# Attention and depthwise convolution, fused: the last image's tail re-planned

## The chip, the cores and the metric

The kernel runs on one core of one Trainium2 chip. The metric is the device time of one execution in microseconds (us); all times here are in us unless ns is written. Engines are called as the profile calls them: PE is TensorE, PEld its weight load, DVE is VectorE, ACT is ScalarE, POOL is GpSimd and SP is SyncE, which here only issues DMAs. L601 is line 601 of the kernel.

## The reference

There are 16 images of 384 channels and 32 x 32 pixels, all float32. Two layers are applied, each as "add to the input":

```
x = x + attention(groupnorm(x))      # 8 heads of 48 channels, 1024 tokens, softmax, projection + bias
x = x + dwconv7x7(groupnorm(x))      # depthwise, weights made symmetric over four rotations, padding 3
```

Group normalization has 32 groups of 12 channels, so each image needs a mean and a variance per group before either layer can start on it. The 7 x 7 depthwise convolution is 49 taps per channel: for each tap the shifted image, times one weight per channel, is added to an accumulator.

## The kernel before

**Layout.** Channels lie on partitions, 128 at a time, so an image is three channel blocks, k = 0, 1, 2, each a tile of 128 x 1024 (32 rows of 32). A tile is written (b, k) here: (14, 2) is block 2 of image 14. `x1[b,k]` is the image after attention and also the accumulator of the convolution; `xn1[b,k]` is its normalized copy, which the taps read.

**Stages.** PE does the attention of image b: q and k (L416), v (L442), scores (L467), weighted sums (L483), projection (L536; in the last image L573). ACT takes the exponentials and evicts. DVE does, meanwhile, the convolution of image b-1 as a chain of taps (L601, one `scalar_tensor_tensor` each). A tile's 49 taps are a *chain*; up to three chains are active and their taps alternate. A program written by hand orders everything: the loop over images issues PE's steps and advances `clock`, an estimate of PE's time; `catch_up(clock)` then places DVE's work until its estimate, `vclock`, has reached `clock`. Due work is kept in a heap (`after(wait, cost, f)`), and what is left of the time is filled with taps, each counted by `us_tap` (L821). Each engine executes its instructions strictly in that order. `us_tap` adds 0.02 to each tap while the last image is in work.

**Statistics for the second normalization.** For images 0 to 13 ACT computes them: `x1_means` (one small DVE instruction, L944), three `Square` activations (`x1_squares`, L265), a gather through DRAM, an aggregate on DVE (L277), `Ln` and `Exp` on ACT, and a spread through DRAM. For image 14 (`ON_VECTOR`, L912) DVE does it: six `bn_stats` (L234), then an aggregate and 14 small instructions (L247 to L222). For image 15, the last, `groups_on_pe` (L290) averages over groups by matmuls with 128 x 1 operands: first `average` of the means (14 PE records, L302), three small DVE instructions (L315 to L317), a second `average` of the variances (14 records), then DVE (L320), POOL's power (L322) and DVE (L323). A callback, `between`, puts one tap on DVE after each average. After that `x1_chains` normalizes the tiles of image 15, (15,2) on DVE, (15,1) on ACT and (15,0) on POOL, and stores two of them to DRAM (`xd`, L676).

**Convolution on PE.** When attention is done PE is free, so some tiles of the last two images (`PE_TILES`) get their taps on PE: (14,2), (14,1), (15,2) and (15,1). The rows come back from DRAM as tiles `sh` (`conv_load`, L683: four DMAs of 160 KB a tile, two tiles for each half of 16 output rows). A half is two pieces (`conv_piece`, L1107) of 56 PE records each (L707): seven taps, four groups of 32 columns side by side, two records per matmul. When a tile is through, DVE adds the result from PSUM (L722). Tile (14,1) is `SHARED`: DVE does its first `SPLIT` = 24 rows and PE the other 8. Tile (15,0) stays on DVE entirely, in two sums (`sum2`, L854), joined at L862. `sh` tiles share a pool of five buffers with `qk`; one of the five holds PE's second set of weights.

**The end of the program.** In the last image the reciprocal of the softmax sums is taken directly (`divide_at_once`, L564, multiply at L565); `fast_finish` then issues the last projection part (L573), adds the residual (L582) and takes `bn_stats`. Then come one piece of (14,2), `fast_end` (the averages and the normalization), and a loop over the pieces that are left: three of (14,2), two of (14,1), four of (15,2), four of (15,1). Before the pieces of image 15 a small matmul checks the softmax sums' range (`check_tensor`, L1093), and DVE reads its result (`good`, L1095). `loads(n)` issues the next `sh` tiles in the order of `pe_loads`, when a piece has ended a half.

Of the kernel before, what the change touches and what calls it, by code (L numbers as in the profile page):

```python
# [44 lines left out]
def kernel(  # L45
# [27 lines left out]
    B, C, H, W = x.shape  # L73
# [36 lines left out]
    def run(general):  # L110
        tag = "g" if general else "f"
        with ExitStack() as stack:
# [24 lines left out]
            xds, shs, pss, mats, psums = {}, {}, {}, {}, {}  # L137
# [1 line left out]

            PE_TILES = [(b, k) for b in (B - 2, B - 1) for k in PE_K]  # L140
            SHARED = None if general else (B - 2, PE_K[1])
            SPLIT = 3 * H // 4
            LONE = (B - 1, 0)

            def flat(t):
# [81 lines left out]
            class Stats:  # L227
# [59 lines left out]
                    )  # L287
                    self.spread(af)

                def groups_on_pe(self, masks, between=lambda: None):  # L290

                    st = small.tile([P, NK, 2], F32, tag="st", name=f"st_{self.name}")
                    for k in range(NK):
                        nc.vector.bn_aggr(st[:, k, :], self.bs[:, k, :])
                    ps = ps_o.tile([P, HALF], F32, tag="acc", name=f"ps_st_{self.name}")

                    def average(c0, src):
                        for mo in range(NK):
                            blocks = [n for n, b in enumerate(MASK_BLOCKS) if b[1] == mo]
                            for n in blocks:  # L300
                                ki = MASK_BLOCKS[n][0]
                                nc.tensor.matmul(  # L302
                                    ps[:, c0 + mo : c0 + mo + 1],
                                    lhsT=masks[:, n, :],
                                    rhs=src[:, ki : ki + 1],
                                    start=(n == blocks[0]),
                                    stop=(n == blocks[-1]),
                                )

                    mean = small.tile([P, NK], F32, tag="mn", name=f"mn_{self.name}")  # L310
                    nc.vector.tensor_copy(mean, st[:, :, 0])
                    average(0, mean)
                    between()
                    d = small.tile([P, NK], F32, tag="d", name=f"d_{self.name}")
                    nc.vector.tensor_tensor(d, mean, ps[:, 0:NK], ALU.subtract)  # L315
                    nc.vector.tensor_tensor(d, d, d, ALU.mult)
                    nc.vector.tensor_tensor(d, d, st[:, :, 1], ALU.add)  # L317
                    average(NK, d)
                    between()
                    nc.vector.tensor_scalar(d, ps[:, NK : 2 * NK], EPS, None, ALU.add)  # L320
                    self.sc = small.tile([P, NK, 2], F32, tag="sc", name=f"sc_{self.name}")
                    nc.gpsimd.tensor_tensor(self.sc[:, :, 0], d, mhalf[:, 0:NK], ALU.pow)  # L322
                    nc.vector.scalar_tensor_tensor(  # L323
                        self.sc[:, :, 1], ps[:, 0:NK], -1.0, self.sc[:, :, 0], ALU.mult, ALU.mult
                    )
# [493 lines left out]
                heapq.heappush(later, (now() + wait, count, cost, f))  # L819

            def us_tap(dy, dx):  # L821
                late_us = 0.02 if clock > last_image else 0.0
                rows = H - abs(dy)
                if tuple(active[0][0:2]) == SHARED:
                    rows = min(H - max(0, dy), SPLIT) - max(0, -dy)
                return (rows * (W - abs(dx)) + (128 if len(active) > 1 else 268)) / 955 + late_us
# [57 lines left out]
            chunks, proj = deque(), deque()  # L884
            ready = {}
            x1_stats = {}
            pe_conv, pe_loads = deque(), deque((bk, h, a) for bk in PE_TILES for h in range(bk == SHARED, 2) for a in range(2))

            def issue(c):
                nonlocal clock  # L890
# [18 lines left out]
            lims = []  # L909

            applies = deque()
            ON_VECTOR = (B - 2,)  # L912

            def project(b):
                nonlocal clock
# [185 lines left out]
            def loads(n):  # L1101
                while n and pe_loads and pe_loads[0][0] in xn1s:
                    (b, k), h, a = pe_loads.popleft()
                    conv_load(b, k, h, a)
                    n -= 1

            def conv_piece():  # L1107
                nonlocal clock
                b, k, h, part = pe_conv.popleft()
                while (b, k, h, 1) not in shs:  # L1110
                    loads(1)
                conv_on_pe(b, k, h, part)
                clock += 3.2 if (b, k) == SHARED else 6.2
                if part == 1:
                    loads(2)
                if (h, part) == (1, 1):
                    after(6.0, 1.2, lambda: conv_on_pe_end(b, k))
# [29 lines left out]
                vclock = clock + 4.0  # L1147

            def fast_end(b):
                x1_stats[b].groups_on_pe(late["masks"], tap)  # L1150
                x1_chains(b, x1_stats[b])

            def once(key, when):
# [5 lines left out]
            for b, n0, size in [  # L1159
                (b, b * PER_B + sum(SIZES[:g]), SIZES[g]) for b in range(B) for g in range(len(SIZES))  # L1160
            ]:
                r = n0 - b * PER_B
                if n0 == NS - PER_B:
                    last_image = clock
                if r % (2 * NT) == 0 and r // (2 * NT) < NK:
                    while chunks and chunks[0][1:] <= (b, r // (2 * NT)):
                        issue(chunks.popleft())
                for n in range(n0, n0 + size):
                    s_step(n)
                clock += (size * US_STEP + US_TURN) / 2  # L1170
                if r == 0:
                    for i in range(NT // 2):
                        issue(("v", b, i))
                ending = b == B - 1 and r + size == PER_B
                if ending:
                    catch_up(clock)
                    divide_at_once(NP * b + NP - 1, 0)
                    vclock += 4.2
                    for o in range(NK):
                        proj_part(b, o, (0, 1))  # L1180
                    clock += 2 * US_PROJ
                else:
                    catch_up(clock)
                    act_slot(4.5)
                    other(n0 + size, False)
                for n in range(n0, n0 + size):
                    av_step(n)
                    u, h, i = n // (2 * NT), n // NT % 2, n % NT
                    if i == NT - 1:
                        take(u, h)  # L1190
                clock += (size * US_STEP + US_TURN) / 2
                if n0 // (2 * NT) < (n0 + size) // (2 * NT):
                    finish((n0 + size) // (2 * NT) - 1)
                if ending:
                    catch_up(clock)
                    assert not invs and not waiting
                    fast_finish(b)
                else:
                    other(n0 + size, True)
                if b == B - 4 and r == 32:  # L1200
                    after(0.0, 2.0, check_early)
                if b == 1 and r == 0:
                    conv_prepare()
                if b == B - 1:

                    if once("mat_0", r >= 16):
                        mat = flat2(xpool.tile([P, NK, N], F32, tag="x", name="mat_0"))
                        conv_matrices(0, mat)
                        late["w3"] = mat[:, 2 * SH * KS * CH :][:, 0:C]
                    if once("w", r >= 32 and b - 1 in x1_stats):  # L1210
                        nc.sync.dma_start(wp, w4[:, 0:NK])
                        nc.sync.dma_start(late["w3"], w4[:, NK])
                    if once("mat_1", r >= 24):
                        conv_matrices(1, flat2(qkpool.tile([P, 2, N], F32, tag="qk", name="mat_1")))
                    if once("ones", r >= 32):
                        t = opool.tile([P, N], F32, tag="o", name="masks_1")
                        nc.sync.dma_start(t, masks.rearrange("p b c -> p (b c)"))
                        late["masks"] = t.rearrange("p (b c) -> p b c", c=P)
                if b == B - 1:
                    if r >= 32 and (b, 0) not in x1s and all(c[0] > b - 2 for c in active):  # L1220
                        for k in range(NK):
                            x1s[b, k] = rpool.tile([P, N], F32, tag="x1", name=f"x1_{b}_{k}")
                            nc.gpsimd.dma_start(
                                x1s[b, k], x[b, k * P : (k + 1) * P].rearrange("p h w -> p (h w)")
                            )
                if b == B - 1 and r in (32, 40, 48):
                    loads(1)
# [63 lines left out]
```

## Time and profile before

| | |
|---|---|
| median of 3 runs | 2943.15 (2942.83 to 2946.42) |
| the profiled execution | 2937.9, of which the span is 2935.8 |
| busy in the span | PE 2905.3, DVE 2572.6, ACT 1435.2, POOL 193.6 |
| last reciprocal (DVE L564) starts | 2828.37 |
| last join of a PE tile (DVE L722) starts | 2922.78 |

Times inside the program are counted from the span's start. The shares of busy time are averages over 16 images; the change lies in the last image and a half, so the timeline there is what has to be read. PE's records in a piece overlap, since the four column groups run side by side.

### The profile page before, as it was taken

The page shows a single profiled execution, that of the slowest core. Times are in us where ns is not written, and L with a number is a line of the kernel's source. Part 1 is how long each engine was busy: PE and PEld are TensorE (multiplying, and loading weights), DVE is VectorE, ACT ScalarE, POOL GpSimd, SP SyncE. Part 2 cuts the span into 40 slices and gives each one's busy share as a digit, 9 for nine tenths or more (in the row PEclk, how much of TensorE's full clock was granted, in tenths as well). Part 3 has the DMA queues.
Part 4 walks back from the last instruction along what each step waited for, and adds up shares of the span by engine and source line. Part 5 has one row for each costly group of instructions (what it writes and reads, how often), then busy time and mean ns, then how long its engine had stood idle before and what let it go on. Part 6 is the DMA issues. An engine that isn't in the chain of part 4 may idle for free. (4 is left out here: it accounts for less than half of the span.)

```text
span 2935.8 us, 30304 instructions
## 1 busy us (share of the span) xinstructions
PE 2905.3 (99%) x11554; PEld 1186.4 (40%) x11554; DVE 2572.6 (88%) x2565; ACT 1435.2 (49%) x1713; POOL 193.6 (7%) x305
## 2 busy tenths in 40 slices
PE   8999999999999999999999999999999999999998
PEld 4343343434434343343434434343343434334335
DVE  4413998989999898989989899898999989899996
ACT  2545445464554545546464554546545365553510
POOL 2113000000100001000000100000010000100000
PEclk9999999999999999999999999999999999999999
DMA  6423022220302213022221301213031221301424
GB/s 234 152 54 70 16 37 68 42 62 23 82 16 42 69 26 79 16 49 55 42 63 26 86 16 35 69 31 73 16 67 38 42 64 26 84 16 35 120 64 111
DMA packets 72540, 169.86 MB, mean 58 GB/s; under 512 B 30416, under 2 KB 32352, under 8 KB 70848
## 3 DMA queue, kind: packets, MB, share of 16 engines
q0 software_dynamic: 29456, 96.10, 13.0%
q1 hardware_dynamic: 41168, 68.12, 9.6%
q10 hardware_dynamic: 1760, 3.61, 0.5%
q8 instruction: 93, 1.52, 0.2%
q14 instruction: 63, 0.52, 0.1%
HBM read 119.93 MB, written 29.36 MB: 51 GB/s over the span
## 5 line engine op out<-in xcount | busy, mean ns | idle before, releaser
L601 DVE SCALAR_TENSOR_TENSOR x<-xn,wsym,x 128x899 f32<-128x899 f32 (+11 forms) x2181 | 2363.9, 1156 | 103.6 <-ACT xn L333 102.7
L475 ACT ACTIVATE e<-ps_s 128x1024 f32<-128x1024 f32 x1024 | 952.4, 1051 | 54.8 <-PE ps_s L467 51.9
L467 PE MATMUL ps_s<-qk 48*128 48x512 f32 x4096 | 915.0, 596 | 1.2 <-ACT qk L423 1.1
L483 PE MATMUL acc<-e,v 128*64 128x512 f32 x4096 | 907.2, 595 | 0.0
L467 PEld LDWEIGHTS ps_s<-qk 48*128 48x128 f32 x4096 | 375.5, 185 | 536.9 <-ACT e L475 259.9
L483 PEld LDWEIGHTS acc<-e,v 128*64 128x64 f32 x4096 | 283.0, 137 | 608.3 <-issue 600.0
L416 PE MATMUL ps_qk<-x,wqk 128*128 128x512 f32 x1152 | 507.1, 596 | 2.4 <-DVE x L329 2.4
L494 ACT COPY o<-acc 128x512 f32<-128x512 f32 x128 | 75.2, 588 | 614.5 <-PE acc L483 614.5
L416 PEld LDWEIGHTS ps_qk<-x,wqk 128*128 128x128 f32 x1152 | 216.8, 190 | 289.0 <-issue 286.5
L442 PE MATMUL ps_v<-wv,x 128*128 128x384 f32 x768 | 252.0, 488 | 0.0
L536 PE MATMUL ps_proj<-o,wp 128*128 128x512 f32 x540 | 234.5, 593 | 0.6 <-DMA o<-o 0.6
L423 ACT COPY qk<-ps_qk 128x1024 f32<-128x1024 f32 x96 | 96.5, 1007 | 248.5 <-PE ps_qk L416 248.4
L442 PEld LDWEIGHTS ps_v<-wv,x 128*128 128x128 f32 x768 | 144.6, 190 | 109.7 <-ACT e L475 12.1
L551 POOL DMA_DIRECT2D x<-in_x x45 | 39.2, 870 | 1864.6 <-ACT x L544 1731.4
L519 DVE TENSOR_TENSOR o<-o,inv 128x1024 f32<-128x1024 f32 x63 | 76.8, 1218 | 88.6 <-DMA inv<-inv 69.7
L536 PEld LDWEIGHTS ps_proj<-o,wp 128*128 128x128 f32 x540 | 102.3, 190 | 127.6 <-issue 123.5
L451 ACT COPY v<-ps_v 128x384 f32<-128x384 f32 x128 | 55.1, 483 | 185.6 <-PE ps_v L442 185.6
L544 ACT ACTIVATE x<-ps_proj,bp 128x1024 f32<-128x1024 f32 x45 | 50.2, 1115 | 184.0 <-PE ps_proj L536 184.0
L333 ACT ACTIVATE xn<-x,sc_x 128x1024 f32<-128x1024 f32 x46 | 53.8, 1231 | 91.2 <-DMA sc_x<-gr_x 62.1
L508 DVE RECIPROCAL rec<-sums 128x16 f32<-128x16 f32 x63 | 15.2, 241 | 77.6 <-DMA sums<-sum 77.6
L707 PE MATMUL ps_conv<-sh,mat 128*32 128x480 f32 (+7 forms) x784 | 78.2, 551 | 1.8 <-DVE good L1095 1.3
L356 DVE BATCH_NORM_STATS2 bs_all<-xs 128x6 f32<-128x512 f32 x84 | 51.9, 679 | 13.5 <-DMA xs<-in_x 13.5
(113 smaller groups left out, 518.5 us busy)
## 6 DMA issues: line engine op xcount, KB each, us to landing
x<-in_x POOLq DMA_DIRECT2D x90, 512.0 KB, 5.6
inv<-inv SPq DMA_DIRECT2D x126, 256.0 KB
out<-x POOLq DMA_DIRECT2D x48, 512.0 KB, 7.4
xs<-in_x POOLq DMA_DIRECT2D x42, 512.0 KB, 6.1
qk<-qk SPq DMA_DIRECT2D x96, 128.0 KB
o<-o SPq DMA_DIRECT2D x90, 64.0 KB
sh<-xd SPq DMA_DIRECT2D x34, 160.0 KB
sh<-xd ACTq DMA_DIRECT2D x22, 160.0 KB
```

The costliest lines, as they stand in the source:

```text
L416: nc.tensor.matmul(ps[:, h, :], lhsT=wqk[:, k, s, t, :], rhs=xns[b][:, k, h * HALF : (h + 1) * HALF], start=(k == 0), stop=(k == NK - 1),)
L423: nc.scalar.copy(halves(qks[u][:, s, :]), ps)
L442: nc.tensor.matmul(ps[:, j, 0:C], lhsT=xns[b][:, k, t * P : (t + 1) * P], rhs=wv[:, k, :], start=(k == 0), stop=(k == NK - 1),)
L451: nc.scalar.copy(dst.rearrange("p (h d) -> p h d", d=D + 1)[:, :, 0:D], ps[:, j, 0:C].rearrange("p (h d) -> p h d", d=D),)
L467: nc.tensor.matmul(ps[:, j, :], lhsT=qks[u][r, 1, i * P : (i + 1) * P], rhs=qks[u][r, 0, h * HALF : (h + 1) * HALF], start=True, stop=True,)
L475: nc.scalar.activation(es[n], ps, AF.Exp, scale=SCALE)
L483: nc.tensor.matmul(accs[u, h][64 * j : 64 * j + 64, :], lhsT=v_of(u, i, j), rhs=e[:, j, :], start=(i == 0), stop=(i == NT - 1),)
L494: nc.scalar.copy(os_[u][:, h * HALF : (h + 1) * HALF], accs.pop((u, h)))
L519: nc.vector.tensor_tensor(os_[u], os_[u], invs.pop(u), ALU.mult)
L536: nc.tensor.matmul(ps[:, h, :], lhsT=wp[:, t, o * P : (o + 1) * P], rhs=os_[NP * b + t][:, h * HALF : (h + 1) * HALF], start=(t == 0), sto ...
L601: nc.vector.scalar_tensor_tensor(acc, xn1s[b, k].rearrange("p (h w) -> p h w", w=W)[:, iy, ix], wsym[:, k, dy + PAD, dx + PAD : dx + PAD + 1],
L707: nc.tensor.matmul(pss[b, k][CH * i : CH * (i + 1), h, :].rearrange("p (y x) -> p y x", x=W)[:, y0:, ox], lhsT=mats[k][:, i, d0 * KS + dx ...
```

## The change

It has five parts. (1) The surcharge per tap in `us_tap` in the last image is 0.045 instead of 0.02, so that the planner counts each tap longer and places fewer of them ahead of each due step. (2) `ON_VECTOR` is empty: image 14's statistics take the way of images 0 to 13, over ACT. (3) `SPLIT` is 28 rows: DVE does 28 rows of tile (14,1) and PE 4. (4) PE's two pieces of (14,1) move: one between the two averages of image 15 (`on_pe`), one right after the second average, ahead of the normalization. (5) The `sh` tiles of (14,1) are loaded first, and a fourth tile is loaded before the last unit's weighted sums (`loads(1)`) and not after it; a planned piece of (14,1) counts 2.0 instead of 3.2.

```
-            SPLIT = 3 * H // 4
+            SPLIT = 7 * H // 8
...
-                def groups_on_pe(self, masks, between=lambda: None):
+                def groups_on_pe(self, masks, between=lambda: None, on_pe=lambda: None):
...
                     average(0, mean)
+                    on_pe()
                     between()
...
-                late_us = 0.02 if clock > last_image else 0.0
+                late_us = 0.045 if clock > last_image else 0.0
...
-            pe_conv, pe_loads = deque(), deque((bk, h, a) for bk in PE_TILES for h in range(bk == SHARED, 2) for a in range(2))
+            pe_conv, pe_loads = deque(), deque(
+                (bk, h, a)
+                for bk in sorted(PE_TILES, key=lambda t: t != SHARED)
+                for h in range(bk == SHARED, 2)
+                for a in range(2)
+            )
...
-            ON_VECTOR = (B - 2,)
+            ON_VECTOR = ()
...
-            def conv_piece():
+            def conv_piece(n=0):
                 nonlocal clock
-                b, k, h, part = pe_conv.popleft()
-                while (b, k, h, 1) not in shs:
+                b, k, h, part = pe_conv[n]
+                del pe_conv[n]
+                while (b, k, h, 1) not in shs and pe_loads:
                     loads(1)
                 conv_on_pe(b, k, h, part)
-                clock += 3.2 if (b, k) == SHARED else 6.2
+                clock += 2.0 if (b, k) == SHARED else 6.2
...
             def fast_end(b):
-                x1_stats[b].groups_on_pe(late["masks"], tap)
+
+                shared = [n for n, c in enumerate(pe_conv) if c[0:2] == SHARED]
+                x1_stats[b].groups_on_pe(late["masks"], tap, lambda: conv_piece(shared[0]))
+                conv_piece(shared[0])
                 x1_chains(b, x1_stats[b])
...
                     for o in range(NK):
                         proj_part(b, o, (0, 1))
+                    loads(1)
                     clock += 2 * US_PROJ
```

In the order of instructions that results, DVE has 72 taps instead of 80 between the multiply of the first pair of heads of image 15 (o60 below, L519) and the last reciprocal, and 43 instead of 29 after it has read `good`. On PE the check and the pieces of image 15 follow directly on (14,2). ACT's queue gets three squares, `Ln`, `Exp` and one small activation of image 14; its four DMA issues for the second half of (14,2) now stand ahead of the normalization of (15,1), and SP's four ahead of the two `xd` stores.

## The prediction

> **What bounds the kernel now.** I read the page first, for the shares, then the timeline of PE and of DVE over the last 120 us, then stage windows there for the granted clock, and last the waits of DVE. The page:
>
> ```profile
> PE 2905.3 (99%) x11554; PEld 1186.4 (40%) x11554; DVE 2572.6 (88%) x2565; ACT 1435.2 (49%) x1713; POOL 193.6 (7%) x305
> ```
>
> PE is the bound for 15 images and the change leaves its work there alone. What it can move is the tail. Timeline of PE (start, length, work, and in brackets the idle time before and what ended it):
>
> ```profile
> 2832.55 6.25 PE L573 MATMUL ps_proj<-o,mat 128*128 128x512 f32 x10 [5.07 <-DVE o L565]
> 2838.73 5.98 PE L707 MATMUL ps_conv<-sh,mat 128*32 128x512 f32 x56
> 2844.64 1.72 PE L302 MATMUL ps_st_x<-mn_x,masks 128*128 128x1 f32 x14
> 2847.01 1.72 PE L302 MATMUL ps_st_x<-d_x,masks 128*128 128x1 f32 x14 [0.64 <-DVE d_x L317]
> 2876.15 46.53 PE L707 MATMUL ps_conv<-sh,mat 128*32 128x512 f32 x448 [1.30 <-DVE good L1095]
> ```
>
> Timeline of DVE:
>
> ```profile
> 2828.37 3.34 DVE L564 RECIPROCAL inv<-ps_sum 128x512 f32<-128x512 f32 x1
> 2909.36 1.23 DVE L862 TENSOR_TENSOR x<-x,sum 128x1024 f32<-128x1024 f32 x1
> 2922.78 1.23 DVE L722 TENSOR_TENSOR x<-ps_conv,x 128x1024 f32<-128x1024 f32 x1 [12.20 <-PE ps_conv L707]
> ```
>
> PE waits 5.07 for a late DVE, its tail follows, and at the end DVE has nothing left and waits 12.20 for PE. So the tail is too long on PE and too short on DVE. The chain of waits shows DVE only, because it ends on DVE's last output; the timeline says that PE ends last. The last join ends at 2924.0; its output and the program's end take 11.8 more, to 2935.8. Windows (PE, PEld, DVE, ACT, POOL busy; granted clock; DMA share; GB/s):
>
> ```profile
> 2827.30:2832.60 5.30, 0.23 (x2) 0.05 (x1) 5.21 (x5) 0.00 (x0) 0.00 (x0) 1.00 0.00 0
> 2832.60:2836.10 3.50, 3.50 (x5) 1.45 (x6) 3.29 (x4) 0.00 (x0) 0.00 (x0) 0.51 0.00 0
> 2842.90:2846.30 3.40, 3.40 (x34) 2.02 (x26) 0.66 (x1) 0.00 (x0) 0.00 (x0) 1.00 0.00 0
> 2846.30:2849.70 3.40, 2.76 (x27) 2.05 (x30) 1.65 (x5) 0.00 (x0) 1.22 (x2) 1.00 0.11 46
> 2849.70:2853.10 3.40, 3.40 (x20) 0.87 (x16) 2.19 (x4) 1.24 (x1) 2.69 (x2) 0.50 0.77 233
> ```
>
> Twice the clock is halved for 3.4, after PE's wait and after the averages: 1.7 of PE's work lost each time.
>
> **Image 14's statistics.** Off DVE go six bn_stats (0.60 from one start to the next, 3.6) and the aggregate with its 14 small steps (2702.73 to 2705.86, 3.1); a small step of 0.1 and an aggregate of 0.4 come. Image 13, whose statistics ACT makes, shows what it becomes; one image is 175.1 (the copy of `o` at 2524.84 and 2699.94):
>
> ```profile
> 2546.75 3.68 DVE L601 SCALAR_TENSOR_TENSOR x<-xn,wsym,x 128x1024 f32<-128x1024 f32 x3 [5.06 <-ACT xn L333]
> 2565.35 1.23 DVE L519 TENSOR_TENSOR o<-o,inv 128x1024 f32<-128x1024 f32 x1 [4.43 <-DMA inv<-inv]
> 2738.29 1.22 DVE L519 TENSOR_TENSOR o<-o,inv 128x1024 f32<-128x1024 f32 x1 [3.03 <-DMA inv<-inv]
> ```
>
> So image 14's first tap starts at 2546.75 + 175.1 = 2721.85, against 2722.69: of 6.2 saved only 0.8 is left, the rest is waiting for ACT. Three taps, a reciprocal and ten taps later (13.4 by the tap rule below) DVE is at 2735.2 and waits for `inv`, which landed at 2738.2. Its DMA stands behind the two `xd` stores, now 3 to 4 later, and behind six qk copies that the copy at 2724.51 holds anyway. Bounds for this multiply, o60: 2738.0, and 2740.4 by image 13's row. I take 2738.6, near this image's own row, since bytes and reciprocal stay where they were. On ACT the squares (1.13 each) push one qk copy by 0.9, and the normalization another by 2.3; image 13 has both and PE does not stall there, so nothing; with that cover gone it would be those 0.9 and 2.3.
>
> **The longer planned tap.** From o60 to the last reciprocal the trace has 90.08. Taps start (elements + 119)/955 us apart: 80 taps 78.1, the 15 other steps 12.1, in all 90.2. Changed: 72 taps, those of (14,1) with 128 elements more, 74.9, and the same 12.1: 86.9. The reciprocal starts at 2738.6 + 86.9 = 2825.5, not 2828.37, and PE has its sum by 2823.2 (L562, 2822.16 + 1.02). With 4.1 to the end of L565, `o` is ready at 2829.65 (before 2832.5). PE then waits about 2.3.
>
> **PE to the check.** From 2829.65: projection 4.3 at full clock (ten records of 0.43), piece of (14,2) 5.9, average 1.7, shared piece S, average 1.7, shared piece S, piece 5.6. The averages do not wait: DVE's mean is due at 2839.85, as PE arrives, and its 0.65 of small steps lies under S. For S the nearest row is the old shared piece, 0.21 a group of four at 256 columns, 28 steps in the two pieces' 5.9. At 128 columns S is 1.5 if columns set it and 3.0 if not; I take 1.6, since 256 columns took exactly half of 512 (0.43). This ends at 2852.1.
>
> [...]
>
> Now a new wait. The second half of (14,2) takes the buffers of (14,1), so its two loads start when the second shared piece ends, 2846.5. Two such tiles issued at 2887.83 kept the DMA engines busy to 2894.2, 6.4; issued at 2868.40 they let PE go at 2876.15, 7.7. That gives 2853.0 to 2854.3; I take 2853.3, a wait of 1.2. The half then takes 11.2 and the check 0.4: 2864.9. Behind these loads on SP stand the `xd` stores, on ACT the normalization of (15,1), held 2; their first readers come at 2865, and from 2888, so that costs nothing. The `xd` bytes also slow the loads: part of the 1.2.
>
> **DVE to the check.** From the second average's end, 2844.9: 1.4 to the scale (before: 2848.73 to 2850.09), 0.7 normalization, 0.2 join, 15 taps 15.2, 1.3 for the limits: 2863.7. So DVE waits 1.2 for PE at `good`: 2865.0.
>
> **The end.** After it DVE has 43 taps, 46.7, two small steps 0.3, three joins of 1.14: 50.4, to 2915.4. PE needs 46.5 for image 15, to 2911.4, its loads being ready (the buffers come free 11 before they are needed). The last join follows on DVE: 2916.6. DVE is the bound then. Of the shared tile's 49 taps x 4 rows (5936 elements, 6.2) all is now on DVE, into the 12.20 that it idled. Against 2924.0 that is 7.4 less; two outputs 1.2 apart do not collide (512 KB move in about 1.3). The profiled execution becomes 2937.9 - 7.4 = 2930.5. The median stands 5.25 above it, and I keep that: 2935.8, 0.25% less. About 0.2%, 5.9, is what a measurement of this kernel can tell from no change.
>
> [...] By the rows a window with 44% of streaming (2825.8 to 2829.2) kept the clock and one with about 30% lost it; a 2.3 gap leaves 31% at worst, the shared pieces among the averages about 47%. My sum takes no drop.
>
> **Rivals.**
> (a) The half clock returns, after the wait for `o` or among the averages. 1.7 each on PE, which DVE pays at `good`: 7.4 becomes 5.7 with one, 4.0 with both, 2937.5 to 2939.2. For it: both drops in the trace; against: shorter gaps. 0.22.
> (b) S near 3.0, or loads near 7.7: PE is 2.8 or 1.0 later at `good`, gain 4.6 to 6.4, 2936.8 to 2938.6. 0.12.
> (c) DVE is not earlier: `inv` of o60 lands as in image 13, 2740.4: gain 5.6, 2937.6. The change's first two parts then mostly do not do what they say. 0.10.
> (d) Slower. The `xd` stores, moved later into the traffic of three outputs and three residual loads of 512 KB, hold o60's `inv` long. Each us past 2738.6 on DVE adds one; from 2746.0 nothing is won. The waits of DVE give the longest:
>
> ```profile
> DVE o L519 <- DMA inv<-inv: 69.7, 26, 16.2
> ```
>
> 16.2 from 2735.2 is 2751.4, a loss of 12.8 - 7.4 = 5.4, to 2948.5; image 13, with such traffic, has 4.43. 0.04.
>
> **How the numbers follow.** Forecast 0.52 at 2935.8, its own range 2934 to 2937: without the wait at the loads and with o60 at 2738.0 it is 1.8 better. (b) and (c) reach above 2937.26 (0.2%) in half of their cases. Faster by over 0.2%: 0.52 + 0.10 = 0.62; slower: 0.04, which I put at 0.05; the rest, 0.33, within. The range reaches from 2933.5 to 2940.5, past both drops of (a) with one of the small costs.
>
> **What would show it.** Right: L564's last reciprocal near 2825.5, PE's idle time before L573 down from 5.07 to about 2.3, full clock throughout, a wait for `sh` of about 1 before the second half of (14,2), `good` near 2865 with PE first, and DVE's last join with no wait for PE. Wrong: o60 past 2741, a clock of 0.5 in a window of 3.4, shared pieces of 3, or a last join that again waits for PE.

## The result: no difference that can be told, and the profile after

| | before | changed | ratio (95%) |
|---|---|---|---|
| median of 6 runs each | 2944.85 (2942.83 to 2947.63) | 2943.43 (2939.81 to 2946.18) | 0.9994 (0.9981 to 1.0006) |
| profiled execution, its span | 2937.9, 2935.8 | 2945.0, 2942.9 | |

The forecast was 2935.8, faster by 0.25%, with a range of 2933.5 to 2940.5. Both are missed: the gain is 1.4, and its interval holds zero.

The two profiled executions can't be laid on each other by their clock times. At the last image's first sum on PE (`ps_sum`, L562 before, L563 after) the changed one is already 5.9 late (2807.89 against 2801.97), and these 5.9 were collected before 290 us, where both programs are the same. In all eleven traces of this study that sum starts between 2801.97 and 2808.60, whatever the kernel. So from here on places in the tail are counted from it: **T+** is the time after that sum's start. By this count the last join ends at T+122.04 before and at T+122.63 after.

Timeline of PE, changed kernel (start, length, work, idle time before and what ended it):

```profile
2839.16 7.46 PE L574 MATMUL ps_proj<-o,mat 128*128 128x512 f32 x10 [5.77 <-DVE o L566]
2846.55 5.98 PE L708 MATMUL ps_conv<-sh,mat 128*32 128x512 f32 x56
2852.46 1.72 PE L302 MATMUL ps_st_x<-mn_x,masks 128*128 128x1 f32 x14
2854.11 1.68 PE L708 MATMUL ps_conv<-sh,mat 128*32 128x128 f32 x56
2855.72 1.72 PE L302 MATMUL ps_st_x<-d_x,masks 128*128 128x1 f32 x14
2857.37 8.10 PE L708 MATMUL ps_conv<-sh,mat 128*32 128x116 f32 x116
2867.16 10.81 PE L708 MATMUL ps_conv<-sh,mat 128*32 128x512 f32 x104 [1.69 <-DMA sh<-xd]
```

PE still waits 5.77 for `o`, more than the 5.07 of before, and the projection behind it takes 7.46, not 4.3. The shared pieces lie between and behind the averages as meant, 1.6 each (2854.11 to 2855.72), and the averages follow without a gap. Then comes the wait for the loads.

Timeline of DVE, changed kernel:

```profile
2728.18 3.36 DVE L602 SCALAR_TENSOR_TENSOR x<-xn,wsym,x 128x1024 f32<-128x1024 f32 x3 [5.99 <-ACT xn L334]
...
2748.18 1.23 DVE L520 TENSOR_TENSOR o<-o,inv 128x1024 f32<-128x1024 f32 x1 [6.64 <-DMA inv<-inv]
...
2878.83 0.15 DVE L1101 TENSOR_REDUCE good<-ps_again 1x1 f32<-1x2 f32 x1 [2.03 <-PE ps_conv L708]
...
2929.30 1.22 DVE L723 TENSOR_TENSOR x<-ps_conv,x 128x1024 f32<-128x1024 f32 x1
```

The end is as forecast: the last join has no wait for PE, where before it had 12.20, so DVE is the bound now. But all in front of it is late. The six us of statistics that left DVE came back as 5.99 of waiting for ACT, and o60's multiply (2748.18) waits 6.64 for `inv`, where it waited 3.03.

Windows of the changed kernel around PE's wait, cut on the clock's own steps (busy PE, PEld, DVE, ACT, POOL; granted clock; DMA share; GB/s):

```profile
2834.80:2838.20 3.40, 0.00 (x0) 0.00 (x0) 3.40 (x2) 0.00 (x0) 0.00 (x0) 1.00 0.00 0
2838.20:2841.60 3.40, 2.44 (x3) 1.18 (x4) 3.15 (x5) 0.00 (x0) 0.00 (x0) 0.50 0.00 0
2841.60:2845.00 3.40, 3.40 (x5) 1.35 (x4) 2.56 (x4) 0.00 (x0) 0.00 (x0) 0.50 0.00 0
```

After a window with nothing on PE the clock is halved for two windows, 6.8: that is the projection's extra 3.1. The drop that before showed behind the averages is gone.

So the loss is on two places: `inv` of o60, and the clock. Why `inv` is late is read on SP's queue. SP's DMA issues, timeline of before (SPq: start, time to issue):

```profile
2716.61 0.85 SPq L676 DMA_DIRECT2D xd<-xn  x2
2717.55 9.14 SPq L432 DMA_DIRECT2D qk<-qk  x6
2726.79 0.59 SPq L510 DMA_DIRECT2D inv<-rec  x1
2733.66 1.12 SPq L513 DMA_DIRECT2D inv<-inv  x2
```

and of the changed kernel:

```profile
2725.91 1.62 SPq L677 DMA_DIRECT2D xd<-xn  x2
2727.62 7.54 SPq L433 DMA_DIRECT2D qk<-qk  x6
2735.26 0.67 SPq L511 DMA_DIRECT2D inv<-rec  x1
2743.29 1.12 SPq L514 DMA_DIRECT2D inv<-inv  x2
```

and SP's waits there (waited for, us in total, times, longest), first before, then changed:

```profile
SPq L432 <- ACT qk L423: 4.6, 1, 4.6
SPq L676 <- ACT xn L333: 0.3, 1, 0.3
```

```profile
SPq L677 <- ACT xn L334: 4.0, 2, 3.3
```

Before, the `xd` stores find `xn` ready; four of the six `qk` copies are issued right behind them, from 2717.55 to 2720.9, and only the last two wait (4.6) for ACT's copy. After, the stores wait 4.0 for ACT's normalization, which itself waits for the statistics to come back through DRAM:

```profile
2724.65 3.50 ACT L334 ACTIVATE xn<-x,sc_x 128x1024 f32<-128x1024 f32 x3 [4.05 <-DMA sc_x<-gr_x]
```

All six copies stand behind the stores and go out in one row, and the issues are longer. Durations of the six issues in ns (shortest, median, longest), first before, then changed:

```profile
L432 SPq DMA_DIRECT2D qk<-qk x6: 507/650/1114, 2717.6 to 2726.1; - x6
L433 SPq DMA_DIRECT2D qk<-qk x6: 632/946/2077, 2727.6 to 2734.4; - x6
```

The late start alone would not have delayed `inv`. At the 3.4 that the first four copies took before, they would have been through at T-76.9 (an estimate: their start, T-80.3, and 3.4), ahead of the end of ACT's last copy, which is T-76.4 in both kernels and holds the last two copies. It is the long issues that push the last two past it. Around them the two stores, three outputs and three residual loads are under way, and the DMA engines move up to 432 GB/s. Their order has changed too: POOL issues the three outputs at T-84.8 to T-83.7, ahead of the stores, where before they left at T-80.9 to T-78.9, behind the stores and those four copies. `inv<-rec` is issued at T-72.6 instead of T-75.2, takes 8.0 instead of 6.9 to the next step, and the multiply is at T-59.70 instead of T-63.68.

### The profile page after: what moved, and what is told of

Same layout as the page of the kernel before. It is cut to its first block, busy times and chain, and to the rows that moved or that the text cites. A ratio compares the mean times of both kernels' runs of the same rounds, so it can differ in the third digit from the quotient of the medians.

```text
span 2942.9 us, 30279 instructions
## 1 busy us (share of the span) xinstructions
PE 2903.6 (99%) x11554; PEld 1172.8 (40%) x11554; DVE 2573.6 (87%) x2546; ACT 1442.1 (49%) x1724; POOL 192.6 (7%) x305
## 5 line engine op out<-in xcount | busy, mean ns | idle before, releaser
L495 ACT COPY o<-acc 128x512 f32<-128x512 f32 x128 | 75.2, 587 | 606.7 <-PE acc L484 606.7
L443 PEld LDWEIGHTS ps_v<-wv,x 128*128 128x128 f32 x768 | 144.6, 190 | 109.6 <-ACT e L476 12.1
L509 DVE RECIPROCAL rec<-sums 128x16 f32<-128x16 f32 x63 | 15.6, 248 | 79.7 <-DMA sums<-sum 79.7
```

The costliest lines, as they stand in the source:

```text
L443: nc.tensor.matmul(ps[:, j, 0:C], lhsT=xns[b][:, k, t * P : (t + 1) * P], rhs=wv[:, k, :], start=(k == 0), stop=(k == NK - 1),)
L495: nc.scalar.copy(os_[u][:, h * HALF : (h + 1) * HALF], accs.pop((u, h)))
```

## The experiments

**Theory**: part 2, image 14's statistics on ACT, turns the `xd` stores into a plug on SP; o60's `inv` comes 3.7 later, PE idles longer for `o`, the clock is halved for two windows, and that eats the gain of parts 3 to 5. **Rivals**: one profiled execution's chance; the planned tap (part 1), whose place matters more; the wait for the loads; contention for DMA bytes whatever SP's order. Places are those of one profiled execution of each kernel; times are medians of 6 to 12 runs, each set beside 6 to 29 runs of the kernel before on the same chip. A window is one step of 3.41 of the granted clock, and a halved one has it at 0.5.

| kernel | o60 | last reciprocal | PE idle for `o`, halved windows behind it | `good` | last join ends | time less that of before | ratio (95%) |
|---|---|---|---|---|---|---|---|
| before | T-63.68 | T+26.40 | 5.07, 1 | T+74.04 | T+122.04 | | |
| before, 2nd trace | T-64.39 | T+25.68 | 4.4, 2 | T+75.40 | T+122.83 | | |
| changed | T-59.70 | T+27.08 | 5.77, 2 | T+70.95 | T+122.63 | -1.4 | 0.9994 (0.9981 to 1.0006) |
| changed, again | T-60.24 | T+26.54 | 5.2, 2 | T+69.17 | T+120.84 | -1.9 | 0.9994 (0.9985 to 1.0002) |
| without part 2 | T-64.28 | T+23.53 | 2.2, 1 | T+65.97 | T+117.63 | -5.2 | 0.9982 (0.9974 to 0.9991) |
| stores behind `inv` | T-63.34 | T+23.79 | 2.5, 0 | T+64.52 | T+116.19 | -5.2 | 0.9983 (0.9974 to 0.9991) |
| part 2 alone | T-59.88 | T+30.20 | 8.9, 3 | T+79.69 | T+128.11 | +3.2 | 1.0009 (1.0000 to 1.0018) |
| without part 1 | T-59.67 | T+30.11 | 8.8, 3 | T+73.67 | T+122.26 | -0.9 | 0.9996 (0.9987 to 1.0005) |
| parts 3 to 5 alone | T-64.33 | T+25.46 | 4.14, 2 | T+69.32 | T+117.91 | -5.9 | 0.9977 (0.9968 to 0.9986) |
| without part 2, wait filled | T-63.49 | T+21.37 | 0.1, 0 | T+61.98 | T+113.65 | -7.9 | 0.9974 (0.9963 to 0.9985) |
| part 3 alone | T-64.10 | T+25.70 | 4.38, 2 | T+74.95 | T+127.22 | +1.5 | 1.0004 (0.9995 to 1.0013) |

Where the idle time has one decimal it is worked out from the starts of PE's records, less 0.59 for the one that runs.

**The two kernels again.** Is it chance? No edit.

> The changed kernel unchanged, for a second trace and more times. All places are counted from the start of PE's first L563 sum of the last image (before 2801.97, changed 2807.89), so that the earlier stages do not matter. Theory (the xd stores moved into other traffic hold o60's inv, and the late DVE halves the clock for two windows): o60's multiply near -59.7 again (before -63.7), its idle time for inv near 6, last reciprocal near +27, the last join near +122.6 (before +122.0); time within 0.1% of before. Rival (chance of one execution): o60 near -63.4 as predicted and the last join near +114.6, time 0.25% less.

> The kernel before, for a second trace. Theory: the 5.9 us by which the first trace of the change was late when the tail begins come from the first 300 us, where both programs are the same, and vary from execution to execution: PE's first L563-like sum (L562 here) starts anywhere from 2801 to 2809, while the last join stays at +122.0 from it, within 1. Rival (the first trace was a lucky one in the tail too): the last join lies 3 or more later than +122.

o60 again waits 6.04 and lies at T-60.24; the second trace of before has it at T-64.39. The last join, at T+120.84, is 1.8 earlier than expected, but far from the T+114.6 of the forecast. The rival of chance falls. The base does move: before's second trace reaches its first sum at 2805.85, 3.9 later than the first one, and its last join lies at T+122.83.

**Without part 2.**

```
-            ON_VECTOR = ()
+            ON_VECTOR = (B - 2,)
```

> The change with image 14's statistics back on VectorE, that part alone undone. Theory: the xd stores go out as early as before, o60's multiply is at -63.7 from PE's first sum as before; 73 taps, 75.9, and 12.1 of other steps follow, the last reciprocal is at +24.3, PE waits 3.0 for o; with no half clock the check is 36.5 after o, near +65, and the last join at +116.6: 5.4 less than before, 2939.5. If the clock is halved for two windows all the same, 3.1 of that is lost: 2942.5. Rival (the loss is at the wait for the loads of the second half of (14,2), not at o60): the last join stays near +122 even with o60 at -63.7. Rival 2 (DVE needs the 6 us that the statistics take): o60 later than -60 and a time above the change's.

o60 is at T-64.28, the reciprocal at T+23.53 (expected +24.3), the time 5.2 less than before. One window of half clock was left, between the two cases of the expectation; so was the last join, 1.0 later than expected. VectorE had room for the statistics: with them it is 4.6 ahead of the changed kernel at o60. The wait for the loads is there too (PE idles 1.47, in the changed kernel 1.69), so it is not what ate the gain. With o60 and PE's wait (2.21) close to where the forecast had them, the clock still fell for one window.

**Only the stores moved.** Statistics stay on ACT; the two stores go on SP behind o60's `inv`.

```
-                        conv_store(b, k)
+                        if b == B - 1:
+                            conv_store(b, k)
+                        else:
+                            after(20.0, 0.0, lambda b=b, k=k: conv_store(b, k))
```

> The change, with the two xd stores of image 14 put on SP behind o60's two inv copies (statistics stay on ScalarE). Theory: inv of o60 no longer waits for the stores' bytes; its first copy is issued 1 to 3 us after the reciprocal instead of 3.8, o60's multiply comes 2 to 4 earlier, near -62.5, the last reciprocal near +24.3, PE's wait near 3, the last join +116 to +118, time 2939 to 2941. Rival (not the stores but the outputs, the residual loads and the slow qk issues hold inv): o60 stays near -59.7 and the time stays that of the change.

SP's issues in this kernel:

```profile
2723.09 10.09 SPq L433 DMA_DIRECT2D qk<-qk  x6
2733.49 0.35 SPq L511 DMA_DIRECT2D inv<-rec  x1
2740.12 1.12 SPq L514 DMA_DIRECT2D inv<-inv  x2
2741.28 1.06 SPq L677 DMA_DIRECT2D xd<-xn  x2
```

The copies begin at T-85.3 (before T-84.4, changed T-80.3), at 0.5 to 0.6 an issue, and only the last two wait, for ACT's copy; `inv<-rec` is at T-74.9, close to before's T-75.2. o60 and the last join come as expected, and the time, 2938.4, is 0.6 below the range named. The first tap of image 14 is even later than in the changed kernel (it waits 8.18 for ACT) and nothing of that reaches the end. This is the same work on every engine as in the changed kernel, in another order on one queue, and 3.3 less in time (5.2 against 1.9, on one chip; the intervals of the two just overlap, while o60 lies at T-63.3 and later than T-60.3 in the two traces of the changed kernel). So the stores' place is the cause of the late `inv`. In all eleven traces the longest issue of these copies goes with it: 2.0 to 2.1 in the four where the stores wait for ACT ahead of the copies, 1.1 in the six where they go out at once, 0.6 here. What makes an issue long isn't shown: the order of the issues and the stores' bytes moved together here, and how the 3.7 divides between them wasn't tried.

**Part 2 alone**, in the kernel before.

```
-            ON_VECTOR = (B - 2,)
+            ON_VECTOR = ()
```

> The kernel before with image 14's statistics on ScalarE, that part of the change alone. Places are counted from PE's first sum of the last image (L562). Theory: the xd stores wait on SP for ScalarE's normalization, and the four qk copies that used to go out before them now stand behind them; inv of o60 is issued 3.8 later, o60's multiply is at -60 instead of -64, the last reciprocal at +29.9 instead of +26.0, PE waits 8.8 for o instead of 5; PE ends last here, so the last join goes from +122.4 to +126 or later: 2947 to 2949, slower. Rival (the 6 us of statistics that VectorE no longer makes are won): o60 at -64 or earlier and 2938 to 2943.

DVE's last join here:

```profile
2931.25 1.23 DVE L722 TENSOR_TENSOR x<-ps_conv,x 128x1024 f32<-128x1024 f32 x1 [12.63 <-PE ps_conv L707]
```

Slower by 3.2, with an interval that just reaches none, as the theory says: o60 waits 7.30 for `inv` and is 3.8 to 4.5 later, paid on PE, which ends last here. The last join lies at T+128.11 (expected +126 or later), with five halved windows in this trace's tail against two and four in those of before.

**Without part 1.**

```
-                late_us = 0.045 if clock > last_image else 0.0
+                late_us = 0.02 if clock > last_image else 0.0
```

> The change without its first part: taps of the last image planned 0.02 longer, as before, not 0.045. 75 taps instead of 72 lie between o60's multiply and the last reciprocal, 40 instead of 43 behind the check. Theory (VectorE's work behind the check sets the end, and moving taps past it only swaps places): o 3 later, PE's wait 9, the check 3 to 5 later, but 3.1 less work after it: last join at +120.5 to +123.5, time that of the change within 0.1%. Rival (the longer planned tap is worth the 3 us by which it brings o forward): last join at +124 to +126, 3 us above the change.

The reciprocal moves from T+27 to T+30.11 and `good` from T+69 to 71 to T+73.67, but only 40 taps are left behind it: T+122.26, and a time within 1 of the change. The longer planned tap brings `o` forward by 3 and hands the same 3 to the end. Where DVE sets the end, moving its taps from one side of a wait to the other wins only what DVE would have idled.

**Parts 3 to 5 alone.**

```
-                late_us = 0.045 if clock > last_image else 0.0
+                late_us = 0.02 if clock > last_image else 0.0
...
-            ON_VECTOR = ()
+            ON_VECTOR = (B - 2,)
```

> The change with its first two parts undone: seven eighths of the shared tile on VectorE and its rest between the averages, alone. Theory: o60 at -64, 75 taps (77.9) and 12.1 later the last reciprocal at +26, PE's wait near 5, half clock for one or two windows, o at +30, the check at +67 to +68.5, then 40 taps, 43.6, and 3.7 of small steps and joins: last join +115 to +117, time 2936 to 2939. So these two parts alone give all of the gain, and more than the whole change. Rival (the longer planned tap is needed with them): 3 us more, 2941 to 2942.

5.9 less than before, at least as good as with part 1 (5.2; the intervals overlap). PE still idled 4.14 for `o` and lost two windows. The last join came 0.9 later than the range named.

**Part 3 alone**, in the kernel before: the split, with PE's rest of the shared tile left behind the averages.

```
-            SPLIT = 3 * H // 4
+            SPLIT = 7 * H // 8
```

> The kernel before with only the split moved from three quarters to seven eighths; the shared tile's rest stays in two pieces behind the averages. Theory: VectorE gets 5936 elements more (6.2), PE loses 28 x 2 groups of half the width, 2.9; VectorE's 33 taps behind the check end under PE's work, so PE still ends last and only its 2.9 count; with half clock behind the averages, if it stays, no more than that: last join at +119 to +120, time 2940 to 2942. So the placing between the averages is worth the other 2 to 3 us of the two parts together (+117.9). Rival (VectorE's share is all that counts): last join at +117.5 to +118, time 2938, and the place of the pieces worth nothing. Rival 2 (the loads of the second half of (14,2) become the wait): last join stays at +122.

All three expectations miss: no gain. Waits of PE in the tail of this kernel:

```profile
PE ps_proj L573 <- DVE o L565: 4.4, 1, 4.4
PE ps_conv L707 <- DVE good L1095: 3.8, 1, 3.8
```

The planner puts 21 taps of DVE between the scale and `good`, one more than before, and PE, through with less work, now waits 3.8 for it, where it waited 1.30. The clock falls three times (from 2831.26, 2848.32 and 2879.04, two windows each). What PE is spared it spends waiting, and the last join still waits 10.95 for PE. So part 3 gains only with parts 4 and 5, which put PE's rest of the shared tile ahead of the normalization and load it first; how much of the gain is part 4's and how much part 5's wasn't tried.

**A version that beats both.** Without part 2, and o60's multiply planned 3.3 later, so that 13 taps and not 10 fill the wait for `inv`:

```
-                after(5.5 if u % NP == NP - 1 else 9.5, 1.3, lambda: finish3(u))
+                after(5.5 if u % NP == NP - 1 else 12.8 if u == U - 4 else 9.5, 1.3, lambda: finish3(u))
```

> The change with image 14's statistics on VectorE, and o60's multiply planned 3.3 later, so that 13 taps instead of 10 fill the wait for inv. Theory: inv still lands at -64.3, VectorE arrives at -65, no wait of over 0.5; 70 taps (73.0) and 12.1 later the last reciprocal is at +21.3, just behind PE's sum; o at +25.5, PE's wait below 1, no half clock, the check at +62, last join at +113.5 to +114.5, time 2935 to 2936. Rival (PE's work up to the check, not VectorE, is the floor, with the loads of the second half of (14,2)): the check not before +64.5, last join +116 as with the stores late, time 2938.

```profile
2745.11 1.23 DVE L520 TENSOR_TENSOR o<-o,inv 128x1024 f32<-128x1024 f32 x1 [0.77 <-DMA inv<-inv]
```

The wait is 0.77, 70 taps are left ahead of the reciprocal, PE goes on to the projection almost without a gap and at full clock, and the last join ends at T+113.65, within the range named; the time, 2936.3, is 0.3 above it. 7.9 less than before, 0.26% (0.15 to 0.37): the gain that was forecast for the change. Against parts 3 to 5 alone, on the same chip, it is 2.0 less, and the intervals overlap.

## Why the prediction was wrong

It forecast the last join's end at 2916.6, T+114.6 by its own trace; it came at T+122.63, 8.0 later. By steps:

1. **The first tap of image 14**, 2721.85 forecast, T-80.1: right, T-79.7. That the saved 6.2 turn into a wait for ACT was seen.
2. **o60's multiply at 2738.6, T-63.4: the step that failed.** It came at T-59.7, +3.7. The prediction had seen the `xd` stores ahead of `inv` and called them 3 to 4 later, and then wrote that the six qk copies are ones "that the copy at 2724.51 holds anyway". So it put the copies' own issue times at nothing. That held before, where only two of them waited for that copy and the other four left SP by 2720.9, in its shadow, at 0.6 to 1.1 each. Behind stores that wait for ACT's normalization the four took 6.1, at up to 2.08 each, ran out of that shadow and put `inv<-rec` 2.6 later; its own way took another 1.2. The place to see the risk was before's own queue: four issues at 2717.55 to 2720.91, two at 2725.55, with 4.6 to spare between them, of which stores 3 to 4 later left about one. How long an issue would then be, no row of before showed (1.1 at most). The reason given for this image's own row, that "bytes and reciprocal stay where they were", left out the issues: image 13's row, 2740.4, was the nearer one, and was not far enough. Rival (c), at 0.10, allowed for 1.8 of these 3.7; rival (d) had the very mechanism, the `xd` stores "moved later into the traffic", and its price, one for one, but at 0.04 and with a loss only from 2746.0 on. o60 came at 2742.3 by before's base, between the two.
3. **o60 to the last reciprocal**, 86.9: right, 86.8 (72 taps of (elements + 119)/955 and 12.1).
4. **PE's wait 2.3, projection 4.3 at full clock: failed**, as step 2's consequence and as rival (a). The wait was 5.77 and the projection 7.46, +3.1. Rival (a) priced one drop at 1.7; it lasted two windows. Nor was "My sum takes no drop" safe with step 2 right: without part 2 PE idled 2.21 and lost one window, with the stores moved it idled 2.46 and lost none. What differed was how much of it fell into one window, 2.16 against 1.70, and nothing in either plan sets that.
5. **Averages and shared pieces**: right. S is 1.6, no wait, no drop. The trace has 56 records in 1.6, 29 ns each at 128 columns, about half of the 53 a record at 256 columns (before's shared pieces, 0.21 a group of four): here the time went with the columns.
6. **The loads of the second half of (14,2)**, mis-sized: from the second shared piece's end, 2859.1, PE goes on at 2867.16, 8.1 and not 6.8, +1.3; all seven traces with this order of pieces have 7.7 to 8.1. Of the two rows at hand it was 7.7 that was near, though by its own bracket (2876.15, `<-DVE good`) that wait ended with `good` and not with the loads; the one of 6.4, the engines' busy time, stopped short of the moment at which PE may go on.
7. **`good` to the end**, 51.6: right, 51.7, with DVE the bound.

3.7 + 3.1 + 1.3 are the 8.0, within 0.1. With steps 2 and 4 put right, the kernel with the stores moved ends at T+116.19, where the forecast with the 1.3 of step 6 has T+115.9: so the mechanisms of the tail were sound, and one queue undid them. What the prediction hung on the whole change belongs to parts 3 to 5, with 5.9; part 1 adds nothing that can be told, and part 2 alone costs 3.2, with an interval that just reaches none.

What the prediction did not see at all is the spread of its base: one trace of before, 2801.97 to the first sum, was the earliest of eleven. It used the differences alone, so this cost it nothing.

## What to carry to other kernels

When an instruction that produces data for a DMA moves later, walk the issuing queue behind that DMA issue by issue, with the start of each: those that used to go out early in the shadow of another wait become part of the path, at whatever an issue then costs (here 0.5 to 1.1 before, up to 2.08 in the changed kernel). Freeing an engine of work in front of a wait that doesn't move wins nothing; filling the wait with work that must be done anyway (13 taps instead of 10) gave the kernel with the lowest median here. And count places in a tail from an event near it when early stages vary by more than the effect.

## What the runs showed of the hardware that was not expected

- **The clock stayed halved after less idle time than it took to halve it.** In the tails of before and of the changed kernel the granted clock keeps a value for 3.41, 13.65, 3.41 and 71.68 (before, from 2832.64) and for 6.82 and 81.92 (changed, from 2838.21), each a whole number of steps of 3.41. From full clock a window of 3.41 with PE idle for 1.75 of it (before, up to 2829.2) or 1.70 (stores behind `inv`) kept the clock, one with 2.16 (without part 2) lost it. But at half clock a window with only 0.8 to 1.2 of idle time was followed by another half one: in the changed kernel (2838.20 to 2841.60, PE busy 2.44), in parts 3 to 5 alone and in before's second trace, while one with no idle time (before, 2832.64) ended it. So an idle time of 4.1 to 5.8 ahead of the projection was followed by one halved window (before) or by two: the projection took 6.25 in before, 7.46 in the changed kernel and 7.54 in parts 3 to 5 alone, where ten records at full clock, 0.43 each, are 4.3. Windows that hold the averages, matmuls of one column, do not fit this: before, one with 0.64 of idle time (up to 2849.70) lost the clock, and in before's second trace one at half clock without any (from 2851.60) was followed by another half one.
- **A DMA issue on SP had no fixed cost here.** The same qk copies took 0.5 to 1.1 each before and up to 2.08 in the changed kernel. The rate of the DMA engines alone doesn't explain it: before's 1.1 (from 2718.28) fell in a stretch at 428 GB/s, the changed kernel's 2.08 (from 2728.84) in one at 264.
- **The first 300 us vary from execution to execution**: the last image's first sum starts anywhere in 6.6 us with all of PE's work ahead of it in the same order, more than the change was to bring.
